# Self-attention's output projection: from seven tiles of full width to three 2 by 2 blocks of seven half-width products and one tile

## The chip, the cores and the metric

The kernel runs on one core of one Trainium2 chip. Time is device time in microseconds (us); the median of three runs is compared. A profiled execution of the same program gives the trace that all readings here come from. Engines: PE does matmuls (PEld is its weight load), DVE, ACT and POOL do elementwise work, SP issues most DMAs. POOL does not work on PSUM in this kernel.

## The reference

One decoder layer on 8 sequences of 112 tokens with 512 features, all in float32. Only the first of its three parts is touched by the change:

```
x = x + attn(layernorm(x))            # 16 heads of 128, causal
    k, q, v = W_K xn, W_Q xn, W_V xn  # per head
    z = softmax(mask(q k^T) / sqrt(128)) v
    attn = W_O z                      # W_O: 512 x 2048, summed over all heads
x = x + cross_attention(layernorm(x), ctx)   # 32 heads of 16, 375 keys
x = x + moe(layernorm(x))                    # 8 experts, 2 chosen, and a shared one
```

## The kernel before, in words

The 896 tokens lie in seven tiles of 128 (`xs[0]` to `xs[6]`, the residual, in SBUF). Sequences 1 to 7 fill rows 0 to 111 of tiles 0 to 6; sequence 0 is cut into seven pieces of 16 that fill the last rows of each tile. So tile t needs the attention output of sequence t + 1 and of sequence 0.

Self-attention runs over four groups `g` of four heads. Each group has these stages, and all engines take their instructions in the order in which a scheduler of the framework put them (it sees the dependencies and its own idea of durations; the order on each engine is fixed when the program is built):

- Queries and keys, `qT` and `kT` (`pair_of_heads`, L262 to L295): seven products of two matmuls with 448 columns for each pair of heads in place of eight. Weight sums for it (`wc`, L266 to L269) are made by POOL, three of the four ahead of time in groups 1 to 3, during the softmaxes of the group before. They rotate through a pool of three buffers, tag "wc".
- Values (`values`, L382 to L427): the generator gives 21 products of two matmuls with 256 columns, in three rounds of seven, from weight sums `wvs` in the same "wc" pool. DVE, ACT and POOL put the products together in four scratch tiles `p1`, `u2`, `p5`, `u3` (pool `up`, two buffers each). Rows that belong to other tiles, or to sequence 0 (`vals[0]`), are sent there by DMAs on SP's queue (L402 to L404, L358).
- Softmax: `softmax(b)` is four score matmuls on PE (L191), scale and mask on DVE (L199), row maximum on DVE (L208), four exponentials on ACT (L211); `normalise` is a reciprocal on DVE (L215) and a multiplication on POOL (L216). `turn` transposes on PE (L222) and copies on ACT (L224, `sT`). `weighted` multiplies with the values on PE (L230, `z`) and copies to `zT` on DVE (L237). Softmaxes and value products are woven together: three value products go with each of the first softmaxes.
- Output projection (`project_o`, L429 to L441): for each tile four matmuls of 512 columns into one PSUM bank, and one DVE addition onto `xs[t]` (L439). In the last group `ln_stats` follows: the statistics of the next layernorm (L142, L143).

PSUM has eight banks in two pools of four: `mm` (values, projection, queries) and `sc` (scores, transposes, weighted values, keys).

After the last group, twelve matmuls for the first keys of cross-attention (L524) stand before the transposes of the second layernorm (L160), which need the statistics of tiles 0 to 3.

The last part of a group in the order of the program:

```
for b in (1, 2, 3, 0, 4):      # softmax(b), three value products each
for b in range(1, B):          # three more products, softmax(b + 4), turn(b + 1), weighted(b)
    if b > 3:
        project_o(b - 4)       # tiles 0 to 3 as their sequences come
for t in range(B - 4, TT - 2): # tile 4; then 5 and 6
```

Of the kernel before, what the change touches and what calls it, by code (L numbers as in the profile page):

```python
# [15 lines left out]
F32 = mybir.dt.float32  # L16
I32 = mybir.dt.int32
AF = mybir.ActivationFunctionType
ALU = mybir.AluOpType
AX = mybir.AxisListType  # L20

P = 128
B, S, D = 8, 112, 512
NT = B * S
TT = NT // P
SP = P - S
ND = D // P
HALF = NT // 2
H, DH = 16, 128
GH = 4  # L30
NG = H // GH
# [28 lines left out]
def seq(ap, b):  # L60

    if b:
        return ap[..., (b - 1) * P : (b - 1) * P + S]
    axes = " ".join("abcd"[: len(ap.shape) - 1])
    return ap.rearrange(f"{axes} (t i) -> {axes} t i", t=TT)[..., S:]


def like_seq(ap, b):

    if b:  # L70
        return ap
    axes = " ".join("abcd"[: len(ap.shape) - 1])
    return ap.rearrange(f"{axes} (t i) -> {axes} t i", t=TT)
# [3 lines left out]
def decoder_layer(  # L77
    ctx: ExitStack, tc: tile.TileContext, x, ctxT, wqk, wv_all, wo, wx, wgate, wsgu, wsd, wegu, wed_a, wed_b, consts, out
):
    nc = tc.nc  # L80
# [7 lines left out]
    mm = ctx.enter_context(tc.tile_pool(name="mm", bufs=4, space=PSUM))  # L88
# [14 lines left out]
    xs = []  # L103
# [13 lines left out]
    def psum(pool, name):  # L117
        return pool.tile([P, 512], F32, tag=pool.name, name=name)
# [18 lines left out]
    def ln_begin(name):  # L137
        return lnpool.tile([P, TT, 2], F32, tag="mv", name=f"mv_{name}")

    def ln_stats(mv, t):  # L140
        st = lnpool.tile([P, 6], F32, tag="st", name="st")
        nc.vector.bn_stats(st, xs[t])  # L142
        nc.vector.bn_aggr(mv[:, t, :], st)  # L143
# [32 lines left out]
    mv2 = ln_begin("2")  # L176
    with ExitStack() as sa:
        wvpool = sa.enter_context(tc.tile_pool(name="weights_vo", bufs=2))
        xcp = sa.enter_context(tc.tile_pool(name="x_sums", bufs=1))
        wcp = sa.enter_context(tc.tile_pool(name="w_sums", bufs=3))  # L180
        up = sa.enter_context(tc.tile_pool(name="part", bufs=2))
# [6 lines left out]
        def softmax(b, qT, kT, q0):  # L188
            ps = psum(sc, "s")
            for h in range(GH):  # L190
                nc.tensor.matmul(  # L191
                    like_seq(ps[:S, h * S : (h + 1) * S], b),
                    qT[:, h, (b - 1) * P : (b - 1) * P + S] if b else q0[:, h, :],
                    seq(kT[:, h, :], b),
                    start=True,
                    stop=True,
                )
            s = sp.tile([S, GH, S], F32, tag="s", name="s", bufs=5)
            nc.vector.scalar_tensor_tensor(  # L199
                out=s,  # L200
                in0=ps[:S, : GH * S].rearrange("q (h p) -> q h p", h=GH),
                scalar=float(DH) ** -0.5,
                in1=mask[:, None, :].to_broadcast([S, GH, S]),
                op0=ALU.mult,
                op1=ALU.add,
            )
            mx = sp.tile([S, GH], F32, tag="mx", name="mx")
            nc.vector.tensor_reduce(mx, s, AX.X, ALU.max, negate=True)  # L208
            sm = sp.tile([S, GH], F32, tag="sm", name="sm")
            for h in range(GH):  # L210
                nc.scalar.activation(s[:, h, :], s[:, h, :], AF.Exp, bias=mx[:, h : h + 1], accum_out=sm[:, h : h + 1])  # L211
            return s, sm

        def normalise(s, sm):
            nc.vector.reciprocal(sm, sm)  # L215
            nc.gpsimd.tensor_tensor(s, s, sm[:, :, None].to_broadcast([S, GH, S]), ALU.mult)  # L216
            return s

        def turn(s):
            pt = psum(sc, "pT")  # L220
            for h in range(GH):
                nc.tensor.transpose(pt[:S, h * S : (h + 1) * S], s[:, h, :], ident[:S, :S])  # L222
            sT = sp.tile([S, GH, S], F32, tag="sT", name="sT")
            nc.scalar.copy(sT, pt[:S, : GH * S].rearrange("p (h q) -> p h q", h=GH))  # L224
            return sT

        def weighted(b, sT, v, zT):
            pz = psum(sc, "z")
            for h in range(GH):
                nc.tensor.matmul(  # L230
                    pz[:, h * S : (h + 1) * S],
                    v[:S, h * DH : (h + 1) * DH],
                    sT[:, h, :],
                    start=True,
                    stop=True,
                )
            nc.vector.tensor_copy(  # L237
                seq(zT, b), like_seq(pz[:, : GH * S].rearrange("p (h q) -> p h q", h=GH), b)
            )
# [58 lines left out]
        for g in range(NG):  # L298
# [11 lines left out]
            wog = wvpool.tile([P, 4, 512], F32, tag="w", name=f"wo_{g}")  # L310
# [9 lines left out]
            qT = qkp.tile([P, GH, NT], F32, tag="qT", name="qT")  # L320
            kT = qkp.tile([P, GH, NT], F32, tag="kT", name="kT")
            zT = zp.tile([P, GH, NT], F32, tag="zT", name="zT")
            for h in range(0, GH, 2):
                for w, dst, pool in ((wq, qT, mm), (wk, kT, sc)):
                    if g == 0 and h == 0 and dst is qT:

                        for half in range(2):
                            cols = bass.ds(half * HALF, HALF)
                            for i in range(2):
                                ps = psum(mm, "qk")  # L330
                                for c in range(ND):
# [4 lines left out]
                                        start=(c == 0),  # L336
                                        stop=(c == ND - 1),
# [10 lines left out]
            soft, turned, vals = {}, {}, {}  # L348
# [20 lines left out]
            wide = D // 2  # L369
# [59 lines left out]
            def project_o(t):  # L429
                ps = psum(mm, "o")  # L430
                for h in range(GH):
                    nc.tensor.matmul(  # L432
                        ps,
                        zT[:, h, t * P : (t + 1) * P],
                        wog[:, h, :],
                        start=(h == 0),
                        stop=(h == GH - 1),
                    )
                nc.vector.tensor_tensor(xs[t], ps, xs[t], ALU.add)  # L439
                if g == NG - 1:  # L440
                    ln_stats(mv2, t)  # L441


            q0 = vp.tile([P, GH, S], F32, tag="q0", name="q0", bufs=1)
            nc.gpsimd.tensor_copy(like_seq(q0, 0), seq(qT, 0))
            values_left()
            products = values()
            for b in (1, 2, 3, 0, 4):
                weights = softmax(b, qT, kT, q0)
                next(products)  # L450
                next(products)
                soft[b] = normalise(*weights)
                next(products)
            turned[1] = turn(soft.pop(1))
            for b in range(1, B):
                for _ in zip(range(3), products):
                    pass
                if b + 4 < B:
                    weights = softmax(b + 4, qT, kT, q0)
                if b + 1 < B:  # L460
                    turned[b + 1] = turn(soft.pop(b + 1))
                if b == 3:
                    turned[0] = turn(soft.pop(0))
                weighted(b, turned.pop(b), vals.pop(b), zT)
                if b == 4:
                    weighted(0, turned.pop(0), vals.pop(0), zT)
                if b + 4 < B:
                    soft[b + 4] = normalise(*weights)
                if b > 3:
                    project_o(b - 4)  # L470
            for t in range(B - 4, TT - 2):
                project_o(t)
            project_o(TT - 2)
            project_o(TT - 1)

# [5 lines left out]
    with ExitStack() as xa:  # L483
# [13 lines left out]
        rawk, rawq, keys, queries, turned = {}, {}, {}, {}, {}  # L497
# [86 lines left out]
        def product(x, w):  # L584
            ps = psum(mm, "kv")
            for c in range(2):
                nc.tensor.matmul(ps[:MC, :], x[:, c, :], w[:, c, :], start=(c == 0), stop=(c == 1))  # L587
            return ps[:MC, :]
# [263 lines left out]
        for b in range(B):  # L852
# [14 lines left out]
            if b + 1 < B:  # L867
# [10 lines left out]
                if b + 2 == B:  # L878
                    sw = [load_shared(i) for i in range(2)]
                    ahead = wpool.tile([P, 4, 512], F32, tag="w", name="ahead")  # L880
# [10 lines left out]
    with ExitStack() as ff:  # L891
# [37 lines left out]
        part = rp.tile([P, NT], F32, name="part")  # L929
# [275 lines left out]
        for i in range(2):  # L1205
            g = gp.tile([P, HALF], F32, tag="g", name="g")
# [20 lines left out]
        h = {}  # L1227
# [109 lines left out]
```

## Time and profile before

| | |
|---|---|
| median of three runs | 1005.09 us (1005.09 to 1005.9) |
| the profiled execution: time | 1005.83 us |
| its span, first to last instruction | 1003.9 us |
| granted TensorE clock, mean | 0.997 |
| PE busy, share of the span | 980.1 us (98%) |
| DVE busy | 408.9 us (41%) |
| ACT busy | 298.2 us (30%) |
| POOL busy | 277.5 us (28%) |

The profiled execution took 1.9 us around its span, and 0.7 us more than the median. Self-attention fills the stretch from the start to about 437.6 us. A busy PE in these tables is not PE at its peak rate, since matmuls overlap and their ends are modelled; the distance from one start to the next is what an instruction costs PE. A float32 matmul of 128 by 128 by 512 appears as two records.

### The profile page before, as it was taken

How to read it: one execution, taken by the hardware profiler on the slowest of the kernel's cores; microseconds unless marked ns; L12 is line 12 of the kernel's file. 1: busy time of each engine (PE TensorE's matmuls, PEld its weight loads, DVE VectorE, ACT ScalarE, POOL GpSimd, SP SyncE). 2: the span in 40 equal slices, each digit the busy share in tenths (PEclk: the TensorE clock that was granted, in tenths of full speed). 3: DMA queues.
4: the chain of work that ended last, by engine and by line, in shares of the span. 5: the costliest groups of instructions: out<-in, count | busy, mean ns of one | idle time of the engine just before them, and what ended most of it. 6: DMA issues, size and time to landing. Idle time of an engine off the chain costs nothing.

```text
span 1003.9 us, 15485 instructions
## 1 busy us (share of the span) xinstructions
PE 980.1 (98%) x5864; PEld 554.7 (55%) x5864; DVE 408.9 (41%) x801; ACT 298.2 (30%) x747; POOL 277.5 (28%) x308
## 2 busy tenths in 40 slices
PE   5999999999999999999999999999999999999998
PEld 3468555954596458645455555555565544444433
DVE  3335223622263235445444454544425243333324
ACT  2135011500152004314354455535543111111100
POOL 4245034603451243122521322222105600000023
PEclk9999999999999999999999999999999999999999
DMA  9522012201211112000001000000209738777765
GB/s 347 199 92 76 2 40 86 62 21 42 84 36 49 42 42 70 14 1 0 31 32 32 2 32 32 32 1 2 85 14 424 263 118 256 236 235 237 215 188 166
DMA packets 35320, 98.85 MB, mean 98 GB/s; under 512 B 4848, under 2 KB 10224, under 8 KB 31664
## 3 DMA queue, kind: packets, MB, share of 16 engines
q1 hardware_dynamic: 30192, 85.26, 25.5%
q0 software_dynamic: 2320, 7.63, 2.3%
q10 hardware_dynamic: 2736, 4.98, 1.6%
q8 instruction: 47, 0.77, 0.3%
q14 instruction: 25, 0.20, 0.1%
HBM read 78.85 MB, written 14.94 MB: 93 GB/s over the span
## 4 chain that ended last, share of the span: by engine, by line
PE 90%; DVE 4%; issue 3%; POOL 1%; DMA 1%; ACT 0%; SPq 0%; DVEq 0%; POOLq 0%; ACTq 0%
PE qk L274 16%; PE kv L587 12%; PE o L432 10%; PE v L393 7%; PE gu L907 5%; PE gate L1143 5%; PE y L1165 4%; PE up L1143 4%; PE xs L751 4%; PE pv L779 4%; PE ys L1191 3%; PE z L230 3%; PE s L191 3%; PE qk L332 1%; PE v L364 1%
## 5 line engine op out<-in xcount | busy, mean ns | idle before, releaser
L762 ACT ACTIVATE e<-xs 125x448 f32<-125x448 f32 x192 | 88.4, 544 | 92.3 <-PE xs L751 92.3
L432 PE MATMUL o<-wo,zT 128*128 128x512 f32 x224 | 99.3, 595 | 0.0
L274 PE MATMUL qk<-xc,wc 128*128 128x448 f32 x180 | 70.1, 539 | 0.0
L432 PEld LDWEIGHTS o<-wo,zT 128*128 128x128 f32 x224 | 41.3, 190 | 46.2 <-issue 45.9
L1176 POOL DMA_INDIRECT got<-routed,at x14 | 15.7, 1118 | 172.4 <-issue 171.2
L587 PE MATMUL kv<-wx,ctx 128*125 128x512 f32 x120 | 56.7, 603 | 0.0
L1143 PE MATMUL gate<-wex,xT 128*64 x144 | 55.3, 466 | 0.5 <-ACT xT L1108 0.5
L907 PE MATMUL gu<-xn,sw 128*128 128x448 f32 x144 | 55.5, 541 | 0.0
L211 ACT ACTIVATE s<-s,mx 112x112 f32<-112x112 f32 x128 | 48.1, 377 | 23.5 <-DVE mx L208 14.9
L1143 PE MATMUL up<-wex,xT 128*64 x144 | 54.3, 459 | 0.0
L274 PEld LDWEIGHTS qk<-xc,wc 128*128 128x128 f32 x180 | 34.2, 190 | 33.5 <-issue 32.3
L751 PE MATMUL xs<-qT,kT 32*125 32x224 f32 x768 | 50.6, 376 | 1.5 <-DVE qT L714 1.5
L1093 DVE COPY xn<-wex 128x704 f32 x60 | 31.2, 524 | 51.2 <-PE up L1143 51.1
L751 PEld LDWEIGHTS xs<-qT,kT 32*125 32x125 f32 x768 | 33.8, 184 | 32.7 <-issue 23.9
L439 DVE TENSOR_TENSOR x<-o,x 128x512 f32<-128x512 f32 x28 | 19.3, 691 | 75.8 <-PE o L432 75.8
L274 PE MATMUL qk<-xn,w 128*128 128x448 f32 x120 | 50.2, 539 | 0.0
L1165 PE MATMUL y<-wd,hT 128*64 128x512 f32 (+1 forms) x216 | 49.5, 593 | 0.6 <-ACT y L1169 0.6
L284 ACT COPY p<-qk 128x448 f32<-128x448 f32 x15 | 8.0, 532 | 137.0 <-PE qk L274 137.0
L216 POOL TENSOR_TENSOR s<-s,sm 112x448 f32<-112x448 f32 x32 | 29.9, 935 | 61.5 <-DVE sm L215 55.6
L506 POOL TENSOR_TENSOR sq<-kraw 125x512 f32<-125x512 f32 x24 | 25.2, 1048 | 78.6 <-DVE kraw L600 19.2
L1143 PE MATMUL gate<-xn,xT 128*64 128x352 f32 x120 | 45.9, 464 | 0.0
L1143 PE MATMUL up<-xn,xT 128*64 128x352 f32 x120 | 45.3, 459 | 0.0
(245 smaller groups left out, 1801.4 us busy)
## 6 DMA issues: line engine op xcount, KB each, us to landing
wd<-in_wed_a SPq DMA_DIRECT2D x27, 512.0 KB, 3.8
wex<-in_wegu SPq DMA_DIRECT2D x8, 1408.0 KB, 19.5
wd<-in_wed_b SPq DMA_DIRECT2D x36, 192.0 KB, 4.7
w<-in_wqk SPq DMA_DIRECT2D x6, 1024.0 KB, 4.9
ctx<-in_ctxT SPq DMA_DIRECT2D x8, 750.0 KB, 4.8
slots<-zeros SPq DMA_DIRECT2D x1, 4608.0 KB, 20.0
wd<-in_wed_a SPq DMA_DIRECT2D x18, 256.0 KB, 4.9
routed<-y SPq DMA_DIRECT2D x18, 256.0 KB, 3.3
```

The source lines that it names most:

```text
L211: nc.scalar.activation(s[:, h, :], s[:, h, :], AF.Exp, bias=mx[:, h : h + 1], accum_out=sm[:, h : h + 1])
L274: nc.tensor.matmul(ps[:, :HALF], wt[:, c * P : (c + 1) * P], x[:, c, :], start=(c == 0), stop=(c == 1))
L393: nc.tensor.matmul(ps[:, :wide], x[:, c, cols], w[:, c, :], start=(c == 0), stop=(c == 1))
L432: nc.tensor.matmul(ps, zT[:, h, t * P : (t + 1) * P], wog[:, h, :], start=(h == 0), stop=(h == GH - 1),)
L587: nc.tensor.matmul(ps[:MC, :], x[:, c, :], w[:, c, :], start=(c == 0), stop=(c == 1))
L751: i = nc.tensor.matmul(strips[j][:MC, ci * 2 * S : (ci + 1) * 2 * S], keys[b][rows, 2 * cp + ci, m * MC : (m + 1) * MC], queries[b][rows, ...
L762: last_exp[(b, cp, m)] = nc.scalar.activation(e[:, :, j, :, :].rearrange("p c e s -> p c (e s)"), strips[j][:MC, : 4 * S].rearrange("p (c ...
L779: nc.tensor.matmul(ps[VW * j : VW * (j + 1), g * S : (g + 1) * S], v[:, m, 16 * cp + h, :], es[m][:, h // 8, (h % 8) // 2, h % 2, :], star ...
L907: nc.tensor.matmul(ps[:, :HALF], w[:, c, i % 2, k, :], xn3[:, c, cols], start=(c == 0), stop=(c == ND - 1))
L1093: nc.vector.tensor_copy(second(j, c), wex[:, bass.ds(moved[j], 1), c, :].rearrange("p o f -> p (o f)"))
L1143: nc.tensor.matmul(gu[k][n, :FF], xT[:, c, n], w, start=(c == 0), stop=(c == ND - 1))
L1165: nc.tensor.matmul(ps[n, :], hT[:fn, i, n], w[i][:fn], start=(i == 0), stop=(i == len(FCH) - 1))
```

## The change

Six of the seven tiles are projected as three pairs (0, 4), (1, 5), (2, 6). A pair is a 2 by 2 block problem: two tiles by two halves of the four heads, times two halves of the heads by two halves of the 512 output columns. It is done in seven products of two matmuls of 256 columns in place of eight such (Strassen's scheme in Winograd's form). Tile 3 is projected as before.

- `output_sums` makes four sums of the group's W_O on POOL, in two buffers of the "wc" pool.
- `project_pair` makes four sums of the two tiles' `zT` on POOL; they are put in the columns of `kT` that the group no longer needs. The first three products need none of these four, the fourth needs `s3`, the fifth `s2`, the sixth `s1`, the seventh `s4`.
- The products are put together by one ACT copy and eight DVE operations of 256 columns in the scratch tiles of pool `up`. Four additions onto `xs` follow, on POOL in the first three groups and on DVE in the last.
- The sequences are taken in the order 1, 5, 0, 2, 6, 3, 7, 4, with five softmaxes ahead and four value products beside each; the remaining product follows at once. A pair is projected as soon as its sequences are done: after sequences 0, 6 and 7.

```diff
+            def output_sums():
+                for i in range(2):
+                    w = wcp.tile([P, 4, wide], F32, tag="wc", name=f"wos{i}")
+                    wos.extend((w[:, 0:2, :], w[:, 2:4, :]))
+                nc.gpsimd.tensor_tensor(wos[0], o12, o11, ALU.subtract)
+                nc.gpsimd.tensor_tensor(wos[1], o22, wos[0], ALU.subtract)
+                nc.gpsimd.tensor_tensor(wos[2], o22, o12, ALU.subtract)
+                nc.gpsimd.tensor_tensor(wos[3], o21, wos[1], ALU.subtract)
+            def project_pair(lo, hi):
...
+                nc.gpsimd.tensor_tensor(s3, a11, a21, ALU.subtract)
+                nc.gpsimd.tensor_tensor(s1, a21, a22, ALU.add)
+                nc.gpsimd.tensor_tensor(s2, s1, a11, ALU.subtract)
+                nc.gpsimd.tensor_tensor(s4, a12, s2, ALU.subtract)
+                def product(x, w):
+                    ps = psum(mm, "o")
+                    for h in range(2):
+                        nc.tensor.matmul(ps[:, :wide], x[:, h, :], w[:, h, :], start=(h == 0), stop=(h == 1))
+                    return ps[:, :wide]
...
+                add = nc.vector.tensor_tensor if g == NG - 1 else nc.gpsimd.tensor_tensor
+                def onto(t, cols, a):
+                    add(xs[t][:, cols], xs[t][:, cols], a, ALU.add)
...
+                nc.scalar.copy(p1, product(a11, o11))
+                nc.vector.tensor_tensor(w, product(a12, o21), p1, ALU.add)
+                onto(lo, left, w)
+                p4 = product(a22, wos[3])
+                nc.vector.tensor_tensor(u3, product(s3, wos[2]), p1, ALU.add)
+                p6 = product(s2, wos[1])
+                nc.vector.tensor_tensor(u3, p6, u3, ALU.add)
+                nc.vector.tensor_tensor(w4, p4, u3, ALU.add)
+                onto(hi, left, w4)
+                nc.vector.tensor_tensor(p1, p6, p1, ALU.add)
+                p5 = product(s1, wos[0])
+                nc.vector.tensor_tensor(p1, p5, p1, ALU.add)
+                nc.vector.tensor_tensor(u3, p5, u3, ALU.add)
+                onto(hi, right, u3)
+                nc.vector.tensor_tensor(p1, product(s4, o22), p1, ALU.add)
+                onto(lo, right, p1)
+                if g == NG - 1:
+                    ln_stats(mv2, lo)
+                    ln_stats(mv2, hi)
...
-            for b in (1, 2, 3, 0, 4):
+            order = (1, 5, 0, 2, 6, 3, 7, 4)
+            ahead = 5
+            for b in order[:ahead]:
                 weights = softmax(b, qT, kT, q0)
                 next(products)
                 next(products)
                 soft[b] = normalise(*weights)
                 next(products)
+                next(products)
             turned[1] = turn(soft.pop(1))
...
+            for _ in products:
+                pass
+            for i, b in enumerate(order):
+                new = order[i + ahead] if i + ahead < B else None
+                if new is not None:
+                    weights = softmax(new, qT, kT, q0)
+                if i + 1 < B:
+                    turned[order[i + 1]] = turn(soft.pop(order[i + 1]))
                 weighted(b, turned.pop(b), vals.pop(b), zT)
...
+                if i == 0:
+                    output_sums()
+                if b in (0, 6, 7):
+                    t = max(b - 5, 0)
+                    project_pair(t, t + 4)
+            project_o(3)
```

More of the change, by code (lines that the diff above doesn't have):

```diff
@@ L441, in project_o @@
                     ln_stats(mv2, t)
+            o11, o12 = wog[:, 0:2, :wide], wog[:, 0:2, wide:]
+            o21, o22 = wog[:, 2:4, :wide], wog[:, 2:4, wide:]
+            wos = []
+            def output_sums():
[6 more added lines that the diff above has]
+                nc.gpsimd.tensor_tensor(wos[3], o21, wos[1], ALU.subtract)
@@ new lines, in project_pair, with part @@
+            def project_pair(lo, hi):
+                z = [zT[:, :, t * P : (t + 1) * P] for t in (lo, hi)]
+                (a11, a12), (a21, a22) = ((t[:, 0:2, :], t[:, 2:4, :]) for t in z)
+                room = kT.rearrange("p h n -> p (h n)")[:, lo * 4 * wide : (lo + 1) * 4 * wide]
+                s1, s2, s3, s4 = (
+                    room[:, k * wide : (k + 1) * wide].rearrange("p (h n) -> p h n", h=2) for k in range(4)
+                )
+                nc.gpsimd.tensor_tensor(s3, a11, a21, ALU.subtract)
[7 more added lines that the diff above has]
+                    return ps[:, :wide]
+                def part(name):
+                    return up.tile([P, HALF], F32, tag=name, name=name)[:, :wide]
+                add = nc.vector.tensor_tensor if g == NG - 1 else nc.gpsimd.tensor_tensor
+                def onto(t, cols, a):
+                    add(xs[t][:, cols], xs[t][:, cols], a, ALU.add)
+                left, right = slice(0, wide), slice(wide, D)
+                p1, w, w4, u3 = part("p1"), part("u2"), part("p5"), part("u3")
+                nc.scalar.copy(p1, product(a11, o11))
[17 more added lines that the diff above has]
+                    ln_stats(mv2, hi)
@@ L453, in decoder_layer @@
                 next(products)
+                next(products)
             turned[1] = turn(soft.pop(1))
[L455 to L463, printed above, removed]
-                weighted(b, turned.pop(b), vals.pop(b), zT)
[L465 to L474, printed above, removed]
+            for _ in products:
[6 more added lines that the diff above has]
+                    turned[order[i + 1]] = turn(soft.pop(order[i + 1]))
+                weighted(b, turned.pop(b), vals.pop(b), zT)
+                if new is not None:
+                    soft[new] = normalise(*weights)
+                if i == 0:
[4 more added lines that the diff above has]
+            project_o(3)
     mv3 = ln_begin("3")
```

## The prediction

> **What bounds the kernel now.** I read the page first (busy shares, granted clock, chain of waits), then the busy times of one group by stage, then the timelines of PE, DVE, ACT and POOL over that group.
>
> ```profile
> PE 980.1 (98%) x5864; PEld 554.7 (55%) x5864; DVE 408.9 (41%) x801; ACT 298.2 (30%) x747; POOL 277.5 (28%) x308
> PEclk9999999999999999999999999999999999999999
> PE 90%; DVE 4%; issue 3%; POOL 1%; DMA 1%; ACT 0%; SPq 0%; DVEq 0%; POOLq 0%; ACTq 0%
> L432 PE MATMUL o<-wo,zT 128*128 128x512 f32 x224 | 99.3, 595 | 0.0
> ```
>
> The end is set by PE (90% of the chain), the clock is never cut, and the projection never waits (its last number, idle before it, is 0.0). A share over the whole span proves little for one stage, so here is one group: softmaxes and values, projection, next queries and keys. The columns are stretch, length, then PE, PEld, DVE, ACT and POOL busy, clock, DMA.
>
> ```profile
> 62.00:97.50 35.50, 35.50 (x229) 31.21 (x228) 20.62 (x45) 20.05 (x80) 18.54 (x25) 1.00 0.29 88
> 97.50:127.00 29.50, 29.50 (x89) 14.75 (x89) 6.62 (x10) 1.29 (x3) 0.15 (x1) 1.00 0.06 16
> 127.00:167.00 40.00, 40.00 (x108) 20.18 (x107) 12.29 (x20) 3.73 (x7) 19.17 (x20) 1.00 0.11 42
> ```
>
> PE is busy in all of each stretch; in the projection DVE has 23 us free of 29.5 and POOL nearly all. PE work taken away there shortens the span, unless it brings a wait. What PE work costs is the distance between starts in PE's timeline (start, duration, engine, line):
>
> ```profile
> 82.60 2.77 PE L393 MATMUL v<-wvs,xc 128*128 128x256 f32 x12
> 85.21 0.95 PE L191 MATMUL s<-kT,qT 128*112 128x112 f32 x8
> ...
> 97.44 3.70 PE L432 MATMUL o<-wo,zT 128*128 128x512 f32 x8
> 100.98 0.60 PE L230 MATMUL z<-sT,v 112*128 112x112 f32 x4
> 101.41 3.61 PE L432 MATMUL o<-wo,zT 128*128 128x512 f32 x8
> 104.86 0.55 PE L222 MATMUL pT<-cst,s 112*112 112x112 f32 x4
> ```
>
> Three half-width value products (two matmuls of 256 columns each) take 85.21 - 82.60 = 2.61 us, 0.87 each. A projected tile takes 104.86 - 101.41 = 3.45 us (3.54 for the first). In the same way four scores cost 0.78, four transposes 0.39, four weighted-value matmuls 0.90.
>
> **PE's saving.** Two tiles: 2 x 3.445 = 6.89 us. A pair in the new form: seven products of exactly the value product's form, 7 x 0.87 = 6.09. So 0.80 a pair, 12 pairs: 9.6 us. All other matmuls stay the same in number and shape.
>
> [...] The row says 0.435 to 0.861, a ratio of 0.505, in the same kernel, type and engine state. I take the row.
>
> **What is added elsewhere.** Prices:
>
> ```profile
> L267 POOL TENSOR_TENSOR wc<-w,wc 128x256 f32<-128x256 f32 x12 | 8.8, 729 | 0.0
> L377 POOL TENSOR_TENSOR wvs<-w 128x512 f32<-128x512 f32 x3 | 3.8, 1269 | 0.0
> L401 DVE TENSOR_TENSOR p<-v,p 128x256 f32<-128x256 f32 x24 | 10.1, 422 | 5.8 <-PE v L393 4.7 <-issue 0.6
> L237 DVE COPY zT<-z 128x448 f32<-128x448 f32 x32 | 19.9, 622 | 6.9 <-PE z L230 6.9
> L727 DVE TENSOR_TENSOR kraw<-kraw,kss x24: 679/684/1204, 452.1 to 721.4; 125x512 f32<-125x512 f32 x24
> ```
>
> POOL, each group: 4 x 1.27 + 12 x 0.73 = 13.8 us, and 12 x 0.73 = 8.8 for the additions onto xs in groups 0 to 2. DVE: 24 x 0.42 + 0.69 in place of 7 x 0.69, +5.9, and +5.0 for the additions in group 3. ACT: three copies, 1.1. All would fit beside PE in sum; what counts is whether each is there in time, which I work out stage by stage, with 0.2 us from PE's end to the reader's start (100.98 to the DVE addition at 101.18).
>
> Sixth softmax to first pair, 0 being the start of the sixth scores (sequence 3). PE: scores 0 to 0.78, transposes of 5, z of 1, scores of 7 until 2.84, transposes of 0, z of 5, scores of 4 until 4.91, transposes of 2, z of 0 from 5.29 to 6.19, transposes of 6, three of z of 2 from 6.57, pair from 7.24. ACT is tight: four exponentials take 1.5 (74.34 to 75.84), a copy of transposes 0.53, and PE gives 2.06 a softmax. Exponentials of 3: 2.3 to 3.8; copy for z of 0: until 4.3, needed 5.29; exponentials of 7: until 5.85; copy for z of 2: until 6.35, needed 6.57; then those of 4. DVE ends the copy of sequence 0 into `zT` at about 7.1, needed 7.24. POOL's normalise of 7 stands in front of the sums and ends at 7.4: s3 8.1, s1 8.8, s2 9.6, s4 10.4; PE wants s3 after three products at 9.85, s2 at 10.7, s4 at 12.5. The ACT copy p1 follows the last exponentials and ends at 8.8; the fifth product needs its bank at 10.7. The seventh needs the bank of the s3 product, which DVE has freed by then, and not that of p4, which DVE still holds.
>
> SP's queue: `vals[0]` must have the last value product's rows before the second half of z of 0, 5.7. The W_O sums stand in front of that product's POOL step (2.5 us), so DVE ends it at about 0.85; the third of its DMAs goes out 2.0 later (90.55 to 92.52) and lands after 1.8, at worst 2.9: 4.7 to 5.7. It just holds. No other DMA is moved past anything that waits; the loads of later weights stay behind these.
>
> Later pairs, 0 being the start of the preceding pair's last product (groups 0 to 2). DVE has six additions to do after the fifth product, the last of them ready at 1.07, then the two copies into `zT`. Pair (1, 5): copies end at 2.0 and 3.2, PE needs the first at 2.37; s3, s1, s2 end at 4.0, 4.7, 5.5, needed 4.98 and 5.85 for s3 and s2. Pair (2, 6): PE arrives at 3.44, sums end at 5.0, 5.7, 6.5, needed 6.05 and 6.92. Nothing waits. Tile 3 has a key product of the next group in front of it (1.5), which covers its copy. POOL's next key sums (`wc`) now come behind the pair: they end some 6 us after the pair's sixth product and are wanted 17.9 after it.
>
> Group 3 has the four additions on DVE, each about as long as a PSUM one (1.08 us for 896 columns at L250). After the fifth product come nine operations at 0.34 to 0.42, and only then the copy of sequence 4: it ends at 3.04, PE stands at 1.77 with nothing else to do: a wait of 1.3. The second pair's s2 comes 0.1 late. Statistics of tile 3 come last; table, reciprocal and normalised row take 3 us after the last matmul and the twelve key matmuls behind it 10.3 (437.64 to 447.94), so the layernorm is covered as before. If that cover were gone it would cost 3 us.
>
> [...]
>
> Margins of 0.1 to 0.3 that I cannot resolve (the copies in front of the first pair, the DMA) get 0.1 a group, 0.4 in all. Bounds: below 0, since the scheduler may have hidden more and PE's 2% idle lies elsewhere, no gain; above, 1 us a group.
>
> **Sum**, against the profiled execution: 1005.83 (span 1003.9 and 1.93 around it) - 9.6 + 1.3 + 0.1 + 0.4 = 998.0. The median is 0.74 below that execution: **997.3**.
>
> **Rivals.** Late sums (A): POOL at its slowest price for this form, 1.04 (the additions at L811 take 0.73 at the median, 1.04 at most). Then s2 of the second and third pair comes 0.5 late, 1.2 a group with the first: 4.8 in all, 1001.7 or so. For: `zT` must be whole before any sum starts. Against: the 0.73 rows come from a stretch in which DVE was as busy.
>
> Serial softmaxes (B), the slower end: the last three have nothing between them but transposes and z, and each z needs an ACT copy that stands behind exponentials. If the chain of each (scores 0.78, DVE 1.3, ACT 1.5, copy 0.53, handovers: 4.3) stood alone, 2.2 us would be lost three times a group: 27 us less 8, 1024. It decides from 0.7 us a softmax on (8.2 / 12). Half of that is 1011. For: the margins of 0.2 above. Against: the last two before stand 2.06 apart too, without a gap on PE.
>
> [...]
>
> **Numbers.** Forecast 0.74 (995.3 to 1000), A 0.11 (0.06 faster, 0.04 the same, 0.01 slower), B 0.12, C 0.03. A measurement of this kernel tells about 0.2%, 2.0 us. Faster 0.80, same 0.04, slower 0.16. The range of 995.2 to 1002.5 holds the forecast and most of A, 0.82.
>
> **What would show it.** The new product's records about 0.87 us apart a product; 24.1 us of projection a group down to 21.7; PE without idle time in groups 0 to 2 and 1.3 us in front of the last tile's projection in group 3; POOL and DVE rows at 0.73 and 0.42. I am wrong if PE waits on POOL in front of the fourth or fifth product, on ACT or DMA in front of z of 0 or 2, or if starts lie over 0.98 us a product apart (6.89 / 7).

## The result, and the profile after

In the first comparison the changed kernel took 993.49 us in the median of four runs (992.4 to 994.56), the kernel before 1005.09 us. The ratio is 0.9891, with a 95% interval of 0.9878 to 0.9904. The forecast was 997.3 us in a range of 995.2 to 1002.5: the change goes the way that was forecast, and the time lies 1.7 us below the range. The profiled execution of the changed kernel took 994.56 us, with a span of 992.7 us.

From its page, and from the groups of instructions, come the lines that answer to those of before (busy shares; chain of waits; then groups with busy time, mean ns, and idle time in front):

```profile
PE 968.1 (98%) x6008; PEld 580.6 (58%) x6008; DVE 432.5 (44%) x885; ACT 302.7 (30%) x759; POOL 357.0 (36%) x408
PE 86%; DVE 4%; issue 4%; POOL 3%; DMA 2%; ACT 0%; POOLq 0%; SPq 0%; DVEq 0%; ACTq 0%
L473 PE MATMUL o<-wos,kT 128*128 128x256 f32 x144 | 33.3, 380 | 0.1
L432 PE MATMUL o<-wo,zT 128*128 128x512 f32 x32 | 14.5, 596 | 1.1 <-DVE zT L237 1.1
```

PE is still the bound. POOL and DVE have taken on 80 and 24 us of work. Two numbers at the ends of the rows are new: the products that read POOL's sums waited 0.1 us in all, and the projection of tile 3 waited 1.1 us for DVE's copy into `zT`.

The busy times of group 0 by stage, of the changed kernel (stretch, length, then PE, PEld, DVE, ACT and POOL busy, clock, DMA): softmaxes and values, then the projections with the next queries and keys.

```profile
60.00:93.04 33.04, 33.04 (x206) 28.82 (x206) 19.11 (x42) 18.15 (x73) 16.86 (x20) 1.00 0.31 93
93.04:161.68 68.64, 68.64 (x252) 43.69 (x251) 24.77 (x50) 8.02 (x21) 42.04 (x52) 1.00 0.10 32
```

PE is busy in all of both: the new sums and additions bring no gap in a full group. What a pair costs is read from the starts in PE's timeline of the changed kernel (start, duration, engine, line):

```profile
93.04 1.91 PE L473 MATMUL o<-wo,zT 128*128 128x256 f32 x8
94.78 1.03 PE L473 MATMUL o<-wos,zT 128*128 128x256 f32 x4
95.65 2.75 PE L473 MATMUL o<-wos,kT 128*128 128x256 f32 x12
98.24 1.03 PE L473 MATMUL o<-wo,kT 128*128 128x256 f32 x4
99.10 0.37 PE L230 MATMUL z<-sT,v 112*128 112x112 f32 x2
```

Seven products take 99.10 - 93.04 = 6.06 us, 0.866 each; the other two pairs of the group take 6.05 and 6.06.

The span fell by 11.1 us. Cut at the same places in both traces, it divides like this (us; the starts are PE's):

| stage | before | after | difference |
|---|---|---|---|
| start to the first value products (L364) of group 0 | 61.83 | 59.83 | -2.00 |
| from there to the same point of group 3 (three groups of 104.48 and of 101.85) | 313.43 | 305.56 | -7.87 |
| from there to the first keys of cross-attention | 62.38 | 61.47 | -0.91 |
| all the rest | 566.23 | 565.87 | -0.36 |

So self-attention's own stages give 8.8 us, and 2.0 us come from a stretch in which the change touches no instruction: on every engine the two programs are the same up to 57 us at least.

### The profile page after: what moved, and what is told of

The parts are those of the page before. It is cut to its first block, busy times and chain, and to the rows that moved or that the text cites. A ratio compares the mean times of both kernels' runs of the same rounds, so it can differ in the third digit from the quotient of the medians.

```text
span 992.7 us, 16065 instructions
## 1 busy us (share of the span) xinstructions
PE 968.1 (98%) x6008; PEld 580.6 (58%) x6008; DVE 432.5 (44%) x885; ACT 302.7 (30%) x759; POOL 357.0 (36%) x408
## 4 chain that ended last, share of the span: by engine, by line
PE 86%; DVE 4%; issue 4%; POOL 3%; DMA 2%; ACT 0%; POOLq 0%; SPq 0%; DVEq 0%; ACTq 0%
PE qk L274 16%; PE kv L652 12%; PE v L393 7%; PE o L473 7%; PE gu L972 5%; PE y L1230 5%; PE gate L1208 5%; PE up L1208 4%; PE xs L816 4%; PE pv L844 4%; PE z L230 3%; PE s L191 3%; PE o L432 1%; PE v L364 1%; POOL sq L571 1%
## 5 line engine op out<-in xcount | busy, mean ns | idle before, releaser
L972 PEld LDWEIGHTS gu<-xn,sw 128*128 128x128 f32 x144 | 26.8, 190 | 24.2 <-issue 24.2
L844 PE MATMUL pv<-e,v 125*32 125x112 f32 x1536 | 40.1, 260 | 0.2
L844 PEld LDWEIGHTS pv<-e,v 125*32 125x32 f32 x1536 | 36.3, 110 | 5.2 <-issue 3.2
L652 PE MATMUL kv<-wx,csum 128*125 128x512 f32 x80 | 38.9, 609 | 0.0
```

The source lines that it names most:

```text
L844: nc.tensor.matmul(ps[VW * j : VW * (j + 1), g * S : (g + 1) * S], v[:, m, 16 * cp + h, :], es[m][:, h // 8, (h % 8) // 2, h % 2, :], star ...
L972: nc.tensor.matmul(ps[:, :HALF], w[:, c, i % 2, k, :], xn3[:, c, cols], start=(c == 0), stop=(c == ND - 1))
```

## Where the two microseconds at the start come from

PE's timeline of the first 25 us, the kernel before and then the changed one:

```profile
9.63 4.07 PE L160 MATMUL ln_t<-cst,xn 128*128 128x128 f32 x16 [9.63 <-DVE xn L153]
14.38 8.53 PE L332 MATMUL qk<-xn,w 128*128 128x448 f32 x16 [0.68 <-ACT xn L161]
```

```profile
9.84 4.07 PE L160 MATMUL ln_t<-cst,xn 128*128 128x128 f32 x16 [9.84 <-DVE xn L153]
14.59 6.28 PE L332 MATMUL qk<-xn,w 128*128 128x448 f32 x16 [0.68 <-ACT xn L161]
```

The transposes are alike. The first sixteen query matmuls take 8.53 us in one execution and 6.28 in the other. Their single starts stand 0.75 us apart until about 19 us in the first, and 0.38 from the second matmul on in the other: in one PE works at half rate for 4.7 us longer. In the trace the records of the granted clock begin at 18.95 and 14.26 us, just where the spacing changes; below, this moment is called the opening. The granted clock of stage tables does not show it: it reads 1.00 in the stretch before the first record too.

The difference lies ahead of everything that the change touches. Whether it belongs to the execution or to the program, the experiments had to show.

**Repeated profiles.** Both kernels were run again unaltered, each in a comparison of five rounds, and then in two single profiles each.

> The kernel before once more, unaltered, for its own spread. Theory 1: single runs lie between 1001.3 and 1005.8 us, and a second profile shows the PE clock opening at another time than 18.95 us, with the first values' start moved by about half of the difference and 104.48 us a group as before. Rival: the start is the same in every run; then the clock opens at 18.95 us and the first values begin at 61.83 us again.

> The changed kernel once more, unaltered. Theory 1: the change itself is worth 8.8 us (the three full groups 2.63 us each and the last 0.91), and what lies above that in the first comparison (11.6 us) is the moment at which the PE clock opened in those runs. Then over more runs the medians lie 8.5 to 10.5 us apart, and a profile with the clock opening at another time than 14.26 us moves only the start of the first values and leaves 101.85 us a group. Rival: all of 11.6 us belongs to the change; then the medians again lie 11 to 12 us apart.

> The kernel before, unaltered, one more profile for the moment at which PE reaches its full rate. So far it lay at 18.2 to 19.0 us in three profiles without the pairs and at 13.3 to 14.3 in four with them, although the instructions of all engines up to there are the same. Theory chance (the moment falls into one of two windows, whatever the program): at least one of these four new profiles lies on the other side. Theory program (something in the changed program sets it): before late, first queries x16 in 8.1 to 8.5 us; after early, 6.3 us.

> The changed kernel, unaltered, one more profile for the same question. Theory chance: the first sixteen query matmuls take 8.1 to 8.5 us in some of these four profiles whichever kernel it is. Theory program: 6.3 us here again.

> The kernel before, unaltered, a further profile for the same question. Theory chance: late or early; theory program: late again, first values near 61.8 us.

> The changed kernel, unaltered, a further profile for the same question. Theory chance: late or early; theory program: early again, first values near 59.8 us.

Measured: the kernel before 1005.2 us (1001.42 to 1006.57, 13 runs; ratio to itself 1.0002, 0.9992 to 1.0012), the changed one 994.6 us (993.68 to 996.41, 5 runs) against 1004.92 us, ratio 0.9905 (0.9891 to 0.9918). The medians lie 10.3 us apart, not 11.6. The four single profiles took 1005.19 and 1004.01 us (before) and 995.07 and 994.68 us (after).

After seven profiles (with those of the variants below) the late opening had come with every kernel without pairs and the early one with every kernel with pairs, which looked like an effect of the program. The two repeated comparisons had changed nothing in this: 18.4 us for the kernel before and 13.9 for the changed one. Three of the four single profiles ended it. This is the same row in the last profile of the kernel before, then in one of the changed kernel:

```profile
14.48 6.28 PE L332 MATMUL qk<-xn,w 128*128 128x448 f32 x16 [0.68 <-ACT xn L161]
```

```profile
14.51 8.31 PE L332 MATMUL qk<-xn,w 128*128 128x448 f32 x16 [0.68 <-ACT xn L161]
```

The kernel before opened at 13.6 us there, the changed kernel at 18.6, and at 18.3 in the other one. So each kernel starts either way: its first values begin near 59.8 us or near 61.7. The stages after the start didn't follow: every profile of the kernel before has 104.48 us a group and every one of the changed kernel 101.85. Over the eleven profiles without a warmed PE, five opened at 13.3 to 14.3 us and six at 18.2 to 19.0.

**Where the two times lie.** In the traces of both first profiles PE stands idle for 0.68 us in front of the first query matmul, which starts at 14.38 us in the kernel before and at 14.59 in the changed one. The changed kernel's opening, at 14.26, falls into this pause; that of the kernel before, at 18.95, comes 4.57 us after its end. What decides between the two times is not shown; each kernel starts either way, so it is not the program alone.

**A warmed PE.** Both kernels with 18 matmuls of the constant ones into a PSUM bank that nothing uses yet, while the first DMAs are under way. Same edit in both:

```diff
+    warm_ps = psum(sc, "warm")
+    for _ in range(18):
+        nc.tensor.matmul(warm_ps[:, :P], ones, ones, start=True, stop=True)
```

> The kernel before with 18 additional matmuls of a tile of ones into an unused bank, from about 1.2 us on, while PE has nothing else to do. Theory 1 (half clock until 18.95 us cost the profiled kernel before 4.7 us, until 14.26 us the kernel after 2.2 us): the first layernorm's transposes start at 9.6 us at full clock, 0.11 us a piece instead of 0.21, and the time falls by 3 to 5 us, to 1000 to 1002. Rival (the late start of the clock is tied to the kernel, by its load or its layout, and more PE work doesn't move it): 1005.

> The changed kernel with the same 18 additional matmuls. Theory 1: the clock is full at the first transposes, and the time falls by 2 us or a little more, to 990 to 991; the difference to the kernel before with the same matmuls is then the change alone, 8.8 to 9.5 us. Rival (the 11.6 us between the medians are all the change's): the difference stays at 11.6.

Measured: before with it 1001.49 us (999.57 to 1004.89, 22 runs), ratio to before 0.9974 (0.9965 to 0.9983); the changed kernel with it 993.03 us (992.39 to 995.44, 5 runs), ratio 0.9894 (0.9877 to 0.9912). The start in PE's timeline of before with warming:

```profile
1.12 6.63 PE L122 MATMUL warm<-ones 128*128 128x128 f32 x36 [1.12 <-DVE ones L111]
12.96 6.28 PE L336 MATMUL qk<-xn,w 128*128 128x448 f32 x16 [0.71 <-ACT xn L165]
```

The clock opens at 6.1 us, the queries run at full rate from their first matmul, and the first values begin at 58.30 us (58.11 in the changed kernel). With the start made alike, the medians lie 1001.49 - 993.03 = 8.5 us apart, beside the 8.8 of the stages. The changed kernel stayed 2 us above the 990 to 991 that had been expected, and the 8.5 is a mixture. Five of the 22 runs of before took 1004.6 to 1004.9 us at a granted clock of 0.994: in these the warming brought nothing, and none of them was profiled. Like with like, at clocks of 0.997 and 0.998, the medians lie 1001.64 - 992.57 = 9.1 us apart (9 runs and 3). The stages' 8.8 us is what the change saves in self-attention; the 2.0 us of the start are not the change's.

Over all eleven times of the unaltered changed kernel, from comparisons on several chips, the median is 994.56 us, still about 10.4 under that of before. A second matter of the clock has a part in the last 1.5 us: a stretch of 3.4 us at half rate near 680 us, shown in the last section. Profiles of the unaltered kernels with it have a mean granted clock of 0.997 or 0.998, those without it 0.999. Of the times with a clock on record, 4 of 74 of the kernel before and 7 of 11 of the changed one have 0.999 or more. Two profiles with a late opening, one of each kernel, have spans 9.9 us apart: 8.8 in self-attention, and 1.2 in the rest, where only the kernel before has the stretch. Each kernel's runs spread over 4.0 to 5.3 us, so how often each kind of execution comes is not settled by these counts.

## The experiments on the projection

**The order alone.** The changed kernel with its new order of sequences, but each pair projected as two full-width tiles, and without any sums.

```diff
-                if i == 0:
-                    output_sums()
                 if b in (0, 6, 7):
                     t = max(b - 5, 0)
-                    project_pair(t, t + 4)
+                    project_o(t)
+                    project_o(t + 4)
```

> The sequences in the new order with four value products beside each softmax, but every tile projected as before, by four matmuls of 512 columns; no pairs, no sums. Theory 1 (the products alone bring the gain inside the groups, 2.6 us of the 8.8 in each of the first three; what is over comes from when PE's clock is granted in full at the start): each group takes 104.5 us from values to values as before, and the time is 1005 us, give or take the 2 us by which the clock's start differs. Rival 2 (the new order takes something away as well, and the products bring only the 0.80 a pair that was forecast): a group takes 104.2 and the time is about 1004. Rival 3 (the order brings waits that the pairs' shorter work hides): over 1007.

Measured: 1006.33 us (20 runs) against 1004.73, ratio 1.0018 (1.001 to 1.0026). Its groups take 104.35 us, between the 104.5 of the first theory and the 104.2 of the second, so the order is worth 0.13 a group and the pairs 104.35 - 101.85 = 2.50, 0.83 a pair. The last group takes 63.64 us instead of 62.38: the order alone costs 1.26 there. PE's timeline of the order alone at the end of that group, and DVE's beside it:

```profile
432.33 1.04 PE L230 MATMUL z<-sT,v 112*128 112x112 f32 x8
434.53 3.70 PE L432 MATMUL o<-wo,zT 128*128 128x512 f32 x8 [1.16 <-DVE zT L237]
```

```profile
432.53 0.69 DVE L439 TENSOR_TENSOR x<-o,x 128x512 f32<-128x512 f32 x1 [1.80 <-PE o L432]
433.25 0.69 DVE L142 BATCH_NORM_STATS2 st<-x 128x6 f32<-128x512 f32 x1
433.86 0.61 DVE L237 COPY zT<-z 128x448 f32<-128x448 f32 x1
```

And the same place in the changed kernel, PE and DVE:

```profile
421.17 1.04 PE L230 MATMUL z<-sT,v 112*128 112x112 f32 x8
423.32 3.70 PE L432 MATMUL o<-wo,zT 128*128 128x512 f32 x8 [1.10 <-DVE zT L237]
```

```profile
422.31 0.42 DVE L483 TENSOR_TENSOR x<-x,p 128x256 f32<-128x256 f32 x1
422.64 0.62 DVE L237 COPY zT<-z 128x448 f32<-128x448 f32 x1
```

From the last weighted values to tile 3's projection pass 2.15 us where 0.89 would do: 1.26 us of wait, as the order alone costs in its last group. There only one addition and one statistics stand in front of the copy, not nine operations. In the changed kernel the weighted values end at 421.17 + 1.04 = 422.21 us and the copy begins at 422.64, so the nine operations hold it up by some 0.4 us. The wait is a matter of the order: the last sequence's `zT` copy has nothing in front of tile 3's projection on PE to hide it. Even with a free DVE, the copy's 0.62 and two handovers of about 0.2 would leave some 0.9 of it (an estimate from these rows).

**Tile 3 earlier.** The changed kernel, with another order in all groups.

```diff
-            order = (1, 5, 0, 2, 6, 3, 7, 4)
+            order = (1, 5, 0, 2, 6, 4, 3, 7)
...
-            project_o(3)
+                if b == 4:
+                    project_o(3)
```

> The changed kernel with the sequences in the order 1, 5, 0, 2, 6, 4, 3, 7: tile 3 is projected after sequence 4, and the pair (2, 6) comes last, so that no matmul stands right behind the copy of the last sequence with nothing in front. Theory 1 (the wait of 1.26 us before the last tile's projection in group 3 comes from nine DVE operations in front of the copy): the wait goes, about 1.2 us less than the changed kernel, 992.2 beside 993.5. Rival (the DVE work is as much as before and the wait only moves to the last pair's sums): no change.

Measured: 994.49 us (992.92 to 995.52, 5 runs), ratio 0.9904 (0.9888 to 0.9919). In time it cannot be told from the changed kernel, and the 992.2 us expected were missed. In the stages it can: the last group takes 60.22 us instead of 61.47, so the wait of 1.25 is gone, and the other groups take 101.99 instead of 101.85, 0.4 us given back in three groups.

**Twice the sums.** How near are POOL's sums to being late? In the changed kernel's POOL timeline the second pair of group 0, and the third like it, are the tightest that still fit:

```profile
101.49 0.72 POOL L465 TENSOR_TENSOR kT<-zT 128x256 f32<-128x256 f32 x1 [0.66 <-DVE zT L237]
102.98 0.73 POOL L467 TENSOR_TENSOR kT<-kT,zT 128x256 f32<-128x256 f32 x1
```

`s2` (L467) ends at 103.71 us, and PE starts the product that reads it at 104.06: at most 0.35 us to spare. In the first pair it is 1.0. Each of the four sums was issued twice:

```diff
-                nc.gpsimd.tensor_tensor(s3, a11, a21, ALU.subtract)
+                for _ in range(2):
+                    nc.gpsimd.tensor_tensor(s3, a11, a21, ALU.subtract)
...
```

> The changed kernel with each of the four sums of a pair done twice on POOL, with the same operands and result. Theory 1: the sums have only about 0.4 us to spare in the pairs of tiles 1 and 5 and of 2 and 6, since the second ends at 103.71 us and PE asks for it at about 104.06; with a copy of each in front the sums in use arrive 1.5 to 2 us late in every pair, so about 5 to 6 us a group and some 20 us in all, near 1014 us. Rival: POOL has room for twice the sums, the projection of a pair waits for nothing; then 993.5 us.

Measured: 1025.04 us (1023.74 to 1025.18, 4 runs), ratio 1.0205 (1.0189 to 1.0221). A group takes 108.81 us instead of 101.85, and the last one 69.58 instead of 61.47: 3 x 6.96 + 8.1 = 29 us. PE's timeline of it, first pair of group 0:

```profile
95.62 1.03 PE L477 MATMUL o<-wos,kT 128*128 128x256 f32 x4
98.50 1.99 PE L477 MATMUL o<-wos,kT 128*128 128x256 f32 x8 [1.85 <-POOL kT L470]
```

PE waits for `s2`, and in the other two pairs for `s3` and `s4` too. With 2.9 us more of POOL work (4 x 0.73) the three pairs of group 0 take 8.17, 8.48 and 8.48 us instead of 6.06: 2.1 to 2.4 of the 2.9 come through. It is more than the 1.5 to 2 that had been expected, and it shows how little cover there is. In the second pair three of the added sums stand in front of `s2`, 2.2 us, and PE loses 1.9 us up to the product that reads it, which leaves the 0.35 us of cover that were read above. In the first pair a normalise of 0.94 us slipped in between the two sums for `s2` as well; PE loses 2.0 of these 3.1 us, so the cover is about 1 us there.

**Both gains together.** Warming, and the earlier tile 3 in the last group alone.

```diff
+    warm_ps = psum(sc, "warm")
+    for _ in range(18):
+        nc.tensor.matmul(warm_ps[:, :P], ones, ones, start=True, stop=True)
...
-            order = (1, 5, 0, 2, 6, 3, 7, 4)
+            order = (1, 5, 0, 2, 6, 3, 7, 4) if g < NG - 1 else (1, 5, 0, 2, 6, 4, 3, 7)
...
-            project_o(3)
+                if b == 4:
+                    project_o(3)
```

> The changed kernel with two edits: 18 matmuls of ones into an unused bank from about 1.2 us, and in the last group alone the value order 1, 5, 0, 2, 6, 4, 3, 7 with tile 3's projection after sequence 4. Theory 1: the wait of 1.26 us in front of tile 3's projection of the last group goes, the other groups keep 101.85 us, and the clock opens near 6 us; the first values start near 58.1 us: span about 989.5, time about 991. Rival: the order costs in the last group what it saves, and the warm clock is given back in the start; then 993.

Measured: 991.52 us (990.3 to 992.04, 4 runs) against 1004.92, ratio 0.9867 (0.9852 to 0.9882), with a span of 989.8 us. The first values begin at 58.10 us, the full groups take 101.85, the last 60.22: both gains stand. At its end, in PE's timeline, the last pair is followed by the keys of cross-attention without a gap:

```profile
423.02 1.03 PE L477 MATMUL o<-wo,kT 128*128 128x256 f32 x4
423.88 10.46 PE L594 MATMUL k<-wx,ctx 128*125 128x512 f32 x24
```

It beats the changed kernel of the same comparison (994.6 us) by 3.1 us.

## Why the prediction was right or wrong

| term | forecast | measured |
|---|---|---|
| twelve pairs | -9.6 | -10.0 (2.50 a group, four groups) |
| new order, full groups | 0 | -0.4 (3 x 0.13) |
| wait before tile 3, group 3 | +1.3 | +1.26 |
| `s2` of the second pair, group 3 | +0.1 | +0.35 |
| margins not resolved | +0.4 | 0 |
| self-attention | -7.8 | -8.8 |
| start | 0 | -2.0 in the profiles compared |
| rest of the kernel | 0 | -0.4 |

- **The step that failed is the clock, which was put at nothing.** The text read "the clock is never cut" from the page's row of clock digits, 25 us a digit, and so took the start and all behind self-attention as fixed. The mean of 0.997 in the table of before spoke against it: 0.003 of 1004 us is 3 us. What the runs showed instead: the profiled execution of before had opened late, at 18.95 us, that of the changed kernel early, at 14.26, and 2.0 us of the difference come from there. So the two profiled times lie 11.3 us apart, not 7.8. A forecast of 8.8 us instead of 7.8, on the median of before, would have given 996.3, inside the range; the clock took the result out of it.
- **What this leaves open for the median.** The 993.49 us stand between runs of 992.56 and 994.42 us, both with a granted clock of 0.999. These went without the stretch at half rate near 680 us that the profiled one has, and no trace shows how they opened. How the start and that stretch share in the median is therefore not shown. That the time lies below the range is not one lucky comparison: the second one gave 994.6 us, 0.6 below it.
- **The saving by PE** was right in kind and nearly in size. The half-width product costs 0.866 us, as the value product did (2.61 us for three), and a pair 6.06 us (6.09 forecast). The row held. That narrow products cost more, the 0.03 of C, no run shows. A pair saves 0.83 in place of 0.80: the product's price had been rounded up to 0.87, and seven of them made 0.03 of it.
- **The allowance of 0.4** for margins that were not resolved was not needed. The scores of the last three softmaxes stand 2.07 us apart (85.79, 87.86, 89.92), no gap comes in front of them (rival B), and POOL's sums take 0.72 to 0.75 us in the mean, not 1.04 (rival A). A was still the nearest: twice the sums cost 29 us.
- **The wait of 1.3 us** before tile 3 was right in size and place. Its cause was only half right: the nine operations were said to make the copy late, but with one addition and one statistics in front of it the wait is as long, and the nine hold the copy up by only some 0.4 us. That the number came out right is in part luck. What decides is that tile 3 comes last with nothing in front of it.
- **The second pair of group 3** came 0.35 late, not 0.1. DVE's, POOL's and PE's timelines of the changed kernel show why:

```profile
406.67 1.28 DVE L142 BATCH_NORM_STATS2 st<-x 128x6 f32<-128x512 f32 x2
407.94 0.59 DVE L237 COPY zT<-z 128x448 f32<-128x448 f32 x1
410.08 0.42 DVE L483 TENSOR_TENSOR x<-x,u 128x256 f32<-128x256 f32 x1
```

```profile
408.61 0.73 POOL L465 TENSOR_TENSOR kT<-zT 128x256 f32<-128x256 f32 x1 [5.64 <-DVE mv L143]
410.10 0.98 POOL L467 TENSOR_TENSOR kT<-kT,zT 128x256 f32<-128x256 f32 x1
```

```profile
410.03 3.10 PE L473 MATMUL o<-wos,kT 128*128 128x256 f32 x12
412.97 1.03 PE L473 MATMUL o<-wo,kT 128*128 128x256 f32 x4
```

The first pair's statistics stand in front of the second pair's copy, so the sums begin late; and `s2` takes 0.98 us instead of 0.73 while DVE adds two SBUF operands (410.08). The three products take 412.97 - 410.03 = 2.94 us instead of 2.59. The first sum ends at 409.34 us, 0.69 before the product that reads it; in the third pair of the group it is 0.98. So the late start takes some 0.3 us of the cover of 0.35 that `s2` has, and its own 0.25 us more come on top. The forecast has no term for sums that take longer beside DVE's additions; these rows show 0.25 us for one. In the last group's other two pairs the first addition onto `xs` meets a sum as well, and there `s4` takes 0.92 us in one and DVE's addition 0.92 instead of 0.42 in the other. That they coincide is seen three times; it was not tested by itself.

## What to carry to other kernels

Compare two profiles first in a stretch that the change cannot touch, here the first 20 us: what differs there belongs to the execution and not to the change, and a few matmul rows (8.53 and 6.28 us for the same sixteen) tell it. Make the sum by stages with the same end points; those gave 8.8 us within a few hundredths in every profile, while the medians moved between 8.5 and 11.6 apart. When a chain of products reads sums made by a slower engine (here POOL, 0.73 us for 256 columns, where DVE takes 0.42), ask how late the first such sum may be and not only how busy the engine is: POOL is busy for 36% of the span, and still has 1 us or less to spare in each pair.

## What the hardware showed that was not expected

- PE's first full rate comes at one of two times, 13.3 to 14.3 us or 18.2 to 19.0 us, with the same instructions in front, and the first values of one kernel begin 1.7 to 2.2 us later in the second case. Eighteen small matmuls from 1.1 us on brought it to about 6 us in the three profiles that have them and let the first values begin 1.2 to 1.7 us sooner than in the early case. What decides between the two times is not shown.
- A stretch of 3.41 us at half clock lies in the middle of 11 of the 14 profiles (their mean granted clock is 0.996 to 0.998, that of the other three 0.999): from 687.96 us on in the kernel before, from 676.44 on in the changed one. The first two lines are the kernel before (busy times by stage; the clock is the first number after the last bracket): in the 3.41 us ahead of the stretch PE was busy for 1.46. The third line is a profile of the changed kernel with a late opening: at the same place of the program PE is busy for 1.81 of 4.00 us, and the clock stays at 1.00.

```profile
684.55:687.96 3.41, 1.46 (x12) 1.12 (x11) 2.66 (x6) 2.74 (x7) 0.34 (x1) 1.00 0.00 0
688.00:691.40 3.40, 3.10 (x21) 2.66 (x24) 0.70 (x2) 1.94 (x4) 0.00 (x0) 0.50 0.02 5
```

```profile
676.00:680.00 4.00, 1.81 (x15) 1.57 (x16) 2.84 (x7) 3.04 (x8) 0.00 (x0) 1.00 0.00 0
```

The page's row of clock digits, 25 us a digit, shows nothing of it. Two profiles of the changed kernel and that of the warmed kernel before had no such stretch, and there cross-attention's scores to the first gate matmul took 317.0 to 317.4 us instead of 318.2 to 319.1: another 1 to 2 us. Of the profiles with a late opening, the four with full-width tiles have the stretch and both of the changed kernel don't. What brings it, and whether a shorter early stage bears on it, is not shown.
